# Dealing TensorE's units by VectorE's load in a graph attention kernel on one Trainium2 core

## The chip, the cores and the metric

The kernel runs on one core of a Trainium2 chip. The metric is the device time of one execution in microseconds (us), lower is better; the number given for a kernel is the median of its runs. Five engines matter: TensorE (PE; its weight loads are listed apart as PEld), VectorE (DVE), ScalarE (ACT), GpSimd (POOL, which here issues all indirect DMAs) and SyncE (SP, which issues plain DMAs).

## The reference

One layer of attention over a sparse graph, with residual and normalisation, all float32. The input x is 16 graphs of 1024 nodes with 512 features; one adjacency matrix of 1024 x 1024 zeros and ones serves all graphs.

```python
q = (x @ Wq + bq).reshape(b, n, H, HD)      # H = 8 heads of 64
k = (x @ Wk + bk).reshape(b, n, H, HD)
v = (x @ Wv + bv).reshape(b, n, H, HD)
scores = einsum('bqhd,bkhd->bhqk', q, k) / sqrt(HD)
scores = scores + (1.0 - adj) * -1e9
attn = softmax(scores, axis=-1)
out = einsum('bhqk,bkhd->bqhd', attn, v).reshape(b, n, d)
y = x + out @ Wo + bo
result = (y - mean(y)) / sqrt(var(y) + 1e-5)
```

Few entries of adj are one, so the kernel works by edges: it gathers the k and v rows of each query's neighbours and never forms the full score matrix.

## The kernel before, in words

**Tiles and blocks.** Queries are sorted by degree and cut into eight tiles of 128 (t = 0 to 7) for each of the 16 graphs ("batches", b). Tile t has OWN[t] own blocks (L27), each holding one neighbour of each of the 128 queries; tiles 6 and 7 have BLOCKS[t] further table blocks (1 and 5, L28) for the queries with more neighbours, whose results are added up by a matmul. Tile 1 (ONE_KEY, L36) holds queries with one neighbour: its attention is the gathered v row itself, so it has no block. A batch has 34 blocks (NBT), the list `blocks` (L934) has 544.

**Places.** The program is written out as places, `n` from -34 to 543 and some beyond (loop at L1165), one block to a place; the order of emission is the order on each engine's queue. In place n, `exponentials(n+3)` (ACT), `products(n+4)` (DVE, L991), the gathers for block n+8 (POOL, L970), `weigh(n+1)` on DVE (L1019) or `weigh(n+2)` on ACT (L1015, eight instructions), `add_own(n)` (DVE, L1031) and `scores(n+4)` (DVE, L995) are emitted. After a tile's last block comes `normalise` (L1043) and then `turn` (L1070), which transposes the tile on PE (L1074) and copies it out on ACT (L1078). Steps that belong to later places are put in `plan` (`later`, early in a place) or `rest` (`later_last`, after ACT's weights).

**TensorE's units.** All projections are cut into units of a known price in us of PE (PRODUCT 0.86 for a 128 x 128 x 512 product; L53). `fronts` is the list of units that make q, k and v of later batches (k and v of a pair of tiles by a seven-product scheme, L746); `finish` (L827) makes the four products with Wo (L629) for a tile that is done. Each place adds `share` to `credit` and units are emitted while credit is positive; a finish goes ahead of fronts, and starts at most once in two places. Inside a batch `share` is a constant (L1177); it is set anew for each place only in the last batches (L1171), and is LAST_SHARE once fronts is empty. What is left of credit is cut to one share (L1239).

**A finish's steps.** After the last product, `out` (L837) adds residual and bias on DVE (L852, L853, the latter with the row sum), and then, by place: `centre` (+1, DVE L858: minus the mean), `spread` (+2, in `rest`; ACT L862: squares around the mean and their sum), `variance` (+3, DVE L865), `power` (+4, POOL L868), `shift` (+5, DVE L871), `norm_out` (+6, ACT L874) and the store (+8, POOL L878). These are the steps while fronts is not empty ("single"); later, two tiles share one power instruction.

**The lead.** In places -34 to -1 the first batch's q, k, v are made while `ranks` (L370) sorts the nodes: row sums of adj on ACT (L382), a key for each node, PE broadcasts the keys (L392), DVE counts smaller keys for one tile of nodes at a time (L405, eight times), shifts the ranks so that the one-edge tile falls on its place (L411 to L417), casts them (L418), and POOL scatters (node, degree) to the table `order` in DRAM by rank (L399, eight indirect DMAs). SP loads the sorted table as `ranked` (L422), DVE casts its first column to `asked_row` (L434), which all later gathers by node use. Then `edges` (L462) makes the lists of neighbours on DVE for each tile. `loads` (L300) fetches weights on ACT's DMA queue and writes zero rows to DRAM from the tiles `zero` and `zeros` (L293, L295), which take both buffers of the tag that q uses (L658).

**Buffers named below.** Tag "qt" has Q_BUFS = 4 buffers, for the gathered query rows of table blocks (L966) and for V1, the v rows of tile 1 (L949). Y_BUFS is 6, and `load_y` (L1206) is held back while five tiles are in flight.

Of the kernel before, what the change touches and what calls it, by code (L numbers as in the profile page):

```python
# [10 lines left out]
F32 = mybir.dt.float32  # L11
# [6 lines left out]
HEADS = 8  # L18
# [12 lines left out]
AHEAD = 8  # L31
KG_BUFS, Q_BUFS, QT_BUFS, PV_BUFS, Y_BUFS = 8, 4, 3, 5, 6
NO_ROW = 65536.0
CODE, ROUND = 2048.0, 12582912.0

LONE, ONE_KEY = 64, 1  # L36

# [126 lines left out]
def kernel(  # L164
# [69 lines left out]
    with ExitStack() as main:  # L234
# [59 lines left out]
        nc.gpsimd.memset(zero, 0.0)  # L294
        zeros = work.tile([P, D], F32, tag="q", name="zeros", bufs=2)  # L295
        nc.gpsimd.memset(zeros, 0.0)
# [3 lines left out]
        def loads():  # L300
# [14 lines left out]
            for i in range(ROWS):  # L315
                nc.scalar.dma_start(kv_rows[i][N:N + 1, 0:D], zero)
                if i:
                    nc.scalar.dma_start(q_rows[i][ds(ONE_KEY * P, P), :], zeros)
            nc.vector.tensor_scalar(before, place[:, 0:P], -1.0, query[:, 0:1], op0=OP.add, op1=OP.is_gt)
# [42 lines left out]
        def later(k, fn):  # L362
            plan.setdefault(now[0] + k, []).append(fn)
# [6 lines left out]
        def ranks():  # L370
# [27 lines left out]
            def scatter(t):  # L398
                nc.gpsimd.indirect_dma_start(  # L399
                    out=order_views[t], out_offset=bass.IndirectOffsetOnAxis(ap=rank_row[:, t:t + 1], axis=0),  # L400
                    in_=asked[:, t, :], in_offset=None,
                )

            for t in range(NT):
                nc.vector.scalar_tensor_tensor(  # L405
                    keys, row, key[:, t:t + 1], place[:, 0:1].to_broadcast([P, N]), op0=OP.is_lt, op1=OP.min, accum_out=rank[:, t:t + 1]
                )
                if t % 3 == 2:
                    yield

            for at, by in ((LONE, LONE), (LONE + P, -LONE - P), (2 * P, P)):  # L411
# [3 lines left out]
                else:  # L415
                    nc.vector.tensor_tensor(moved, moved, key, op=OP.add)
            nc.vector.tensor_tensor(rank, rank, moved, op=OP.add)  # L417
            nc.vector.tensor_copy(rank_row, rank)  # L418
            for t in range(NT):
                scatter(t)  # L420
            yield
            nc.sync.dma_start(ranked, order.rearrange("(t p) c -> p t c", p=P))  # L422
            nc.vector.tensor_scalar(key, query, 1.0, None, op0=OP.add)
            nc.vector.scalar_tensor_tensor(key, rank, CODE, key, op0=OP.mult, op1=OP.add)
            nc.vector.tensor_copy(keys.rearrange("p (t q) -> p t q", t=NT), key[:, :, None].to_broadcast([P, NT, P]))
# [401 lines left out]
        def finish(b, t):  # L827
# [9 lines left out]
            def out(p):  # L837
# [18 lines left out]

                def centre():
                    nc.vector.tensor_scalar(st[:, 1:2], st[:, 0:1], -1.0 / D, None, op0=OP.mult)  # L858

                def spread():  # L860
                    sq = work.tile([P, D], F32, tag="ysq", name=f"ysq_{b}_{t}", bufs=1)
                    nc.scalar.activation(sq, y, AF.Square, bias=st[:, 1:2], accum_out=st[:, 2:3])  # L862

                def variance():
                    nc.vector.tensor_scalar(st[:, 2:3], st[:, 2:3], 1.0 / D, EPS, op0=OP.mult, op1=OP.add)  # L865

# [3 lines left out]
                def shift():  # L870
                    nc.vector.tensor_tensor(st[:, 4:5], st[:, 3:4], st[:, 1:2], op=OP.mult)  # L871

# [10 lines left out]

                later(1, centre)
                later_last(2, spread)
                later(3, variance)
                if single:
                    later(4, power)
                    later(5, shift)
                    later_last(6, norm_out)  # L890
                elif second:
                    mate_shift, mate_norm_out = half.pop()[1]

# [12 lines left out]
                    later_last(7, norm_out)  # L906
                else:
                    mine = half[0]
                    mine.append((shift, norm_out))
# [34 lines left out]
        def gather(n):  # L944
            b, t, i = blocks[n]
            assert t in listed
            if t == ONE_KEY + 1 and i == 0:
                g = NS + own[ONE_KEY]
                V1[b] = work.tile([P, D], F32, tag="qt", name=f"v1_{b}", bufs=Q_BUFS)  # L949
                nc.gpsimd.indirect_dma_start(  # L950
                    out=V1[b], out_offset=None, in_=kv_rows[b % ROWS],
                    in_offset=bass.IndirectOffsetOnAxis(ap=keys_of(b)[:, g:g + 1], axis=0), element_offset=D,
                )
# [188 lines left out]

        total = len(blocks)
        prep = {}
        for t in range(NT):
# [5 lines left out]
        with tc.manual_schedule():  # L1151
# [13 lines left out]
            while n < total or plan or rest or urgent or done or finishing or spilled or not guarded:  # L1165
# [25 lines left out]
                if 1 <= n <= total and (n == total or blocks[n][2] == 0):  # L1191
                    normalise(*blocks[n - 1][:2])
                if 0 <= n < total and blocks[n][1:] == (ONE_KEY + 1, 1):
                    turn(blocks[n][0], ONE_KEY, V1.pop(blocks[n][0]))
# [4 lines left out]
                for fn in rest.pop(n, ()):  # L1199
                    fn()  # L1200
                credit += share
                if 0 <= n < total and blocks[n][2] >= OWN[blocks[n][1]]:
# [10 lines left out]
                while credit > 0 or urgent:  # L1213
# [68 lines left out]
```

## Time and profile before

| | us |
|---|---|
| median of 3 runs | 1985.66 |
| lowest and highest | 1980.79, 1988.05 |
| the profiled execution, own time | 1981.95 |
| its span, first to last instruction | 1980.2 |

| engine | busy us | share of the span | instructions |
|---|---|---|---|
| PE | 1878.0 | 95% | 5271 |
| DVE | 1746.8 | 88% | 3727 |
| ACT | 1544.4 | 78% | 6074 |
| POOL | 1282.8 | 65% | 1206 |

The mean granted TensorE clock is 0.987. The chain of work that ended last lies 58% on PE, 19% on DVE, 6% on ACT. A float32 product is recorded as two matmul records of 512 columns. A record's duration has a modelled end that reaches into the next one, so that 95% is not a share of the peak; the step from one record's start to the next in an unbroken row is what it costs.

### The profile page before, as it was taken

The numbers are of one execution on the slowest core, as the hardware profiler recorded it, in microseconds if no ns is written. First come the engines' busy times: TensorE is split into PE (matmuls) and PEld (weight loads), VectorE is DVE, ScalarE is ACT, GpSimd is POOL, SyncE is SP. The second block draws the span as 40 slices with busy tenths as digits, with TensorE's granted clock in tenths as the row PEclk, the third lists the DMA queues.
The fourth block names the chain that finished last, engine by engine and source line by source line (L and its number), as shares of the span: only waits on it lengthen the run. The fifth ranks groups of instructions, "written<-read, shape, count | busy, mean of one in ns | idle before, by whom it ended". The sixth has DMA issues, their size and how long they took to land.

```text
span 1980.2 us, 25432 instructions
## 1 busy us (share of the span) xinstructions
PE 1878.0 (95%) x5271; PEld 904.0 (46%) x5271; DVE 1746.8 (88%) x3727; ACT 1544.4 (78%) x6074; POOL 1282.8 (65%) x1206
## 2 busy tenths in 40 slices
PE   8879899999999999999999999999999999899896
PEld 4434444444544445454544445454544445444442
DVE  3599988989988998998989899998989899989894
ACT  4514887979878897978888797887879798978784
POOL 1554665767658675776758576776857576656783
PEclk9989999999999999999999999999999999999998
DMA  7598787888878787897979788897978789987983
GB/s 267 161 310 281 240 284 260 274 289 288 314 245 301 253 306 271 272 330 247 324 222 312 266 286 301 290 312 239 314 245 297 266 291 325 323 293 266 343 315 115
DMA packets 186003, 551.29 MB, mean 278 GB/s; under 512 B 31247, under 2 KB 31275, under 8 KB 185838
## 3 DMA queue, kind: packets, MB, share of 16 engines
q0 software_dynamic: 120528, 398.76, 61.4%
q1 hardware_dynamic: 62416, 145.30, 19.4%
q10 hardware_dynamic: 2894, 5.52, 0.8%
q14 instruction: 121, 0.99, 0.2%
q8 instruction: 44, 0.72, 0.2%
HBM read 433.86 MB, written 140.30 MB: 290 GB/s over the span
## 4 chain that ended last, share of the span: by engine, by line
PE 58%; DVE 19%; ACT 6%; issue 5%; DMA 3%; POOL 1%; POOLq 0%; DVEq 0%; ACTq 0%
PE po L629 15%; PE pq L629 12%; PE pp L746 9%; PE z L746 7%; PE x L746 7%; DVE qk L991 4%; ACT pv L1015 4%; DVE s L995 4%; DMA kvg<-kv_rows,key_row 2%; PE poT L1074 2%; DVE pv L1031 2%; PE pxT L600 2%; PE sum L1040 2%; PE sum L1041 2%; DVE y L853 1%
## 5 line engine op out<-in xcount | busy, mean ns | idle before, releaser
L1015 ACT ACTIVATE pv<-kvg,pv 128x64 f32<-128x64 f32 x3544 | 893.1, 340 | 0.0
L970 POOL DMA_INDIRECT kvg<-kv_rows,key_row x544 | 622.0, 1143 | 388.5 <-ACT pv L1005 118.1
L629 PE MATMUL po<-wo,oT 128*128 128x512 f32 x944 | 434.6, 596 | 5.5 <-DVE y L852 5.5
L629 PE MATMUL pq<-wq,xT 128*128 128x512 f32 x904 | 426.9, 599 | 4.8 <-DVE y L852 2.4
L995 DVE TENSOR_REDUCE s<-qk 128x8 f32<-128x512 f32 x544 | 370.4, 681 | 6.9
L991 DVE TENSOR_TENSOR qk<-qt,kvg 128x512 f32<-128x512 f32 x448 | 306.9, 685 | 13.0 <-DMA kvg<-kv_rows,key_row 12.9
L629 PEld LDWEIGHTS po<-wo,oT 128*128 128x128 f32 x944 | 176.4, 191 | 209.2 <-issue 192.0
L629 PEld LDWEIGHTS pq<-wq,xT 128*128 128x128 f32 x904 | 168.5, 192 | 194.3 <-issue 174.9
L746 PE MATMUL pp<-t,s 128*128 128x512 f32 x504 | 238.7, 596 | 7.9 <-DVE s L615 7.8
L746 PE MATMUL x<-b,xT 128*128 128x512 f32 x504 | 240.3, 599 | 0.0
L1031 DVE TENSOR_TENSOR pv<-pv,pv 128x520 f32<-128x520 f32 x336 | 233.6, 695 | 2.6 <-ACT pv L1015 2.6
L1005 ACT ACTIVATE pv<-s,absent 128x8 f32<-128x8 f32 x448 | 131.0, 294 | 66.7 <-DVE s L995 65.6
L800 POOL DMA_INDIRECT x<-in_x_dram,asked_row x120 | 128.9, 1074 | 78.7 <-PE pxT L600 42.5
L878 POOL DMA_INDIRECT out_dram<-y,asked_row x128 | 148.9, 1163 | 36.4 <-issue 20.5
L639 ACT ACTIVATE sq_k<-kv 128x128 f32<-128x128 f32 x512 | 150.8, 301 | 18.6 <-DVE kv L769 18.6
L1078 ACT COPY oT<-poT 128x512 f32<-128x512 f32 x128 | 73.8, 577 | 104.8 <-PE po L629 99.0
L746 PEld LDWEIGHTS pp<-t,s 128*128 128x128 f32 x504 | 94.7, 191 | 120.5 <-issue 108.7
L746 PEld LDWEIGHTS x<-b,xT 128*128 128x128 f32 x504 | 96.5, 193 | 113.9 <-issue 109.5
L800 POOL DMA_INDIRECT y<-in_x_dram,asked_row x102 | 115.4, 1131 | 31.1 <-issue 26.3
L746 PE MATMUL z<-b,s 128*128 128x512 f32 x252 | 122.1, 608 | 13.0 <-DVE kv L774 13.0
L940 POOL DMA_INDIRECT qg<-q_rows,query_row x96 | 104.1, 1084 | 36.1 <-issue 24.3
L746 PE MATMUL pp<-t,xT 128*128 128x512 f32 x252 | 118.5, 592 | 1.7 <-DVE q L659 1.7
(221 smaller groups left out, 2663.9 us busy)
## 6 DMA issues: line engine op xcount, KB each, us to landing
kv_rows<-kv SPq DMA_DIRECT2D x128, 512.0 KB
q_rows<-q SPq DMA_DIRECT2D x113, 256.0 KB
qt<-q_rows SPq DMA_DIRECT2D x105, 256.0 KB
kvg<-kv_rows,key_row POOLq DMA_INDIRECT x544, 6.0
residual<-y_sorted SPq DMA_DIRECT2D x26, 256.0 KB
y<-residual SPq DMA_DIRECT2D x26, 256.0 KB
adj<-in_adj_dram POOLq DMA_DIRECT2D x8, 512.0 KB, 11.9
spill<-oT SPq DMA_DIRECT2D x10, 256.0 KB
```

Of the source, the lines that this page charges most:

```text
L629: nc.tensor.matmul(p, lhs(c), w[:, c, :], start=(c == 0), stop=(c == NPAIR - 1))
L639: nc.scalar.activation(sq, s[:, ts(h, P)], AF.Square, scale=scale, accum_out=sums[:, h:h + 1])
L746: nc.tensor.matmul(R[bank], l[:, ts(c, P)], right[:, c, :], start=(first and c == 0), stop=(c == 1), skip_group_check=True,)
L800: nc.gpsimd.indirect_dma_start(out=y, out_offset=None, in_=x_rows, in_offset=bass.IndirectOffsetOnAxis(ap=asked_row[:, t:t + 1], axis=0), ...
L878: nc.gpsimd.indirect_dma_start(out=out_rows[b, t], out_offset=bass.IndirectOffsetOnAxis(ap=asked_row[:, t:t + 1], axis=0), in_=y, in_offse ...
L940: nc.gpsimd.indirect_dma_start(out=q, out_offset=None, in_=q_rows[b % ROWS], in_offset=bass.IndirectOffsetOnAxis(ap=rows, axis=0))
L970: nc.gpsimd.indirect_dma_start(out=KG[n], out_offset=None, in_=kv_rows[b % ROWS], in_offset=bass.IndirectOffsetOnAxis(ap=keys_of(b)[:, g:g ...
L991: nc.vector.tensor_tensor(QK[n], q, KG[n][:, 0:D], op=OP.mult)
L995: nc.vector.tensor_reduce(S[n], QK.pop(n).rearrange("p (h d) -> p h d", d=HD), axis=AX.X, op=OP.add)
L1005: nc.scalar.activation(PV[n][:, D:], S.pop(n), AF.Exp, bias=bias)
L1015: nc.scalar.activation(pv[:, ts(h, HD)], v[:, ds(D + h * HD, HD)], AF.Copy, scale=pv[:, D + h:D + h + 1])
L1031: nc.vector.tensor_tensor(PV[b, t], PV[b, t], pv, op=OP.add)
```

## The change

1. The one-edge tile's V1 is gathered with block (7, 0) of its batch in place of (2, 0), and turned in the place of block (7, 4) in place of (2, 1). Q_BUFS goes from 4 to 5.
2. In places 0 to 543, `credit` gets `paced(share, n)` in place of `share`: share times the load of the place over the mean load of its batch. The load counts VectorE's large instructions of the attention in that place: 2 for products and scores, 1 if the next block is weighed on DVE, 1 for add_own, and for a tile's first block 3 or 1.3 for the normalisation of the tile before. The rest of credit is cut to two shares.
3. `centre` is gone. `spread` takes the row sum itself as its bias with scale -512 and moves from +2 to +1; `variance` divides by 512 cubed, `shift` divides the sum by -512 in one three-operand instruction. While fronts is not empty, variance stays at +3, power at +4, shift goes from +5 to +6, norm_out from +6 to +7; once it is empty, single tiles do variance, power, shift and norm_out one place sooner than before (+2, +3, +4, +5).
4. In `ranks`, each tile's ranks are cast and scattered right after the next tile's count; the table in DRAM then lies in plain rank order, and the move of the one-edge tile is made by loading `ranked` in four DMAs. The shift of the ranks for the code follows afterwards.
5. `zeros` moves from q's tag to the tag "pv0".

```diff
-KG_BUFS, Q_BUFS, QT_BUFS, PV_BUFS, Y_BUFS = 8, 4, 3, 5, 6
+KG_BUFS, Q_BUFS, QT_BUFS, PV_BUFS, Y_BUFS = 8, 5, 3, 5, 6
-LONE, ONE_KEY = 64, 1
+LONE, ONE_KEY, ONE_KEY_AT = 64, 1, (7, 4)
-        zeros = work.tile([P, D], F32, tag="q", name="zeros", bufs=2)
+        zeros = work.tile([P, D + HEADS], F32, tag="pv0", name="zeros", bufs=3)
...
                 nc.vector.scalar_tensor_tensor(
                     keys, row, key[:, t:t + 1], place[:, 0:1].to_broadcast([P, N]), op0=OP.is_lt, op1=OP.min, accum_out=rank[:, t:t + 1]
                 )
+                if t:
+                    nc.vector.tensor_copy(rank_row[:, t - 1:t], rank[:, t - 1:t])
+                    scatter(t - 1)
                 if t % 3 == 2:
                     yield
+            nc.vector.tensor_copy(rank_row[:, NT - 1:NT], rank[:, NT - 1:NT])
+            scatter(NT - 1)
+            yield
+            nc.sync.dma_start(ranked[:, 2:, :], order[2 * P:, :].rearrange("(t p) c -> p t c", p=P))
+            nc.sync.dma_start(ranked[0:LONE, 0, :], order[0:LONE, :])
+            nc.sync.dma_start(ranked[LONE:, 0, :], order[LONE + P:2 * P, :])
+            nc.sync.dma_start(ranked[:, ONE_KEY, :], order[LONE:LONE + P, :])
...
-            nc.vector.tensor_tensor(rank, rank, moved, op=OP.add)
-            nc.vector.tensor_copy(rank_row, rank)
-            for t in range(NT):
-                scatter(t)
-            yield
-            nc.sync.dma_start(ranked, order.rearrange("(t p) c -> p t c", p=P))
+            nc.vector.tensor_tensor(moved, rank, moved, op=OP.add)
...
-                def centre():
-                    nc.vector.tensor_scalar(st[:, 1:2], st[:, 0:1], -1.0 / D, None, op0=OP.mult)
-
                 def spread():
...
-                    nc.scalar.activation(sq, y, AF.Square, bias=st[:, 1:2], accum_out=st[:, 2:3])
+                    nc.scalar.activation(sq, y, AF.Square, bias=st[:, 0:1], scale=-float(D), accum_out=st[:, 2:3])
...
                 def shift():
-                    nc.vector.tensor_tensor(st[:, 4:5], st[:, 3:4], st[:, 1:2], op=OP.mult)
+                    nc.vector.scalar_tensor_tensor(
+                        st[:, 4:5], st[:, 0:1], -1.0 / D, st[:, 3:4], op0=OP.mult, op1=OP.mult
+                    )
...
-                later(1, centre)
-                later_last(2, spread)
-                later(3, variance)
+                later_last(1, spread)
                 if single:
-                    later(4, power)
-                    later(5, shift)
-                    later_last(6, norm_out)
+                    late = 1 if fronts else 0
+                    later(2 + late, variance)
+                    later(3 + late, power)
+                    later(4 + 2 * late, shift)
+                    later_last(5 + 2 * late, norm_out)
                 elif second:
+                    later(3, variance)
...
-            if t == ONE_KEY + 1 and i == 0:
+            if (t, i) == (ONE_KEY_AT[0], 0):
...
+        def load_of(n):
+
+            b, t, i = blocks[n]
+            had = 2.0 + (not by_act(min(n + 1, total - 1))) + (0 < i < OWN[t])
+            if i == 0:
+                had += 3.0 if BLOCKS[blocks[n - 1][1]] else 1.3
+            return had
+
+        def paced(share, n):
+            b0 = min(n // NBT, B - 1) * NBT
+            return share * load_of(n) * NBT / sum(load_of(m) for m in range(b0, b0 + NBT)) if n < total else share
...
-                if 0 <= n < total and blocks[n][1:] == (ONE_KEY + 1, 1):
+                if 0 <= n < total and blocks[n][1:] == ONE_KEY_AT:
                     turn(blocks[n][0], ONE_KEY, V1.pop(blocks[n][0]))
...
-                credit += share
+                credit += paced(share, n) if n >= 0 else share
...
-                credit = min(credit, share)
+                credit = min(credit, 2 * share)
```

More of the change, by code (lines that the diff above doesn't have):

```diff
@@ L317, in loads @@
                 if i:
-                    nc.scalar.dma_start(q_rows[i][ds(ONE_KEY * P, P), :], zeros)
+                    nc.scalar.dma_start(q_rows[i][ds(ONE_KEY * P, P), :], zeros[:, 0:D])
             nc.vector.tensor_scalar(before, place[:, 0:P], -1.0, query[:, 0:1], op0=OP.add, op1=OP.is_gt)
@@ L416, in ranks @@
                     nc.vector.tensor_tensor(moved, moved, key, op=OP.add)
-            nc.vector.tensor_tensor(rank, rank, moved, op=OP.add)
-            nc.vector.tensor_copy(rank_row, rank)
-            for t in range(NT):
-                scatter(t)
-            yield
-            nc.sync.dma_start(ranked, order.rearrange("(t p) c -> p t c", p=P))
+            nc.vector.tensor_tensor(moved, rank, moved, op=OP.add)
             nc.vector.tensor_scalar(key, query, 1.0, None, op0=OP.add)
-            nc.vector.scalar_tensor_tensor(key, rank, CODE, key, op0=OP.mult, op1=OP.add)
+            nc.vector.scalar_tensor_tensor(key, moved, CODE, key, op0=OP.mult, op1=OP.add)
             nc.vector.tensor_copy(keys.rearrange("p (t q) -> p t q", t=NT), key[:, :, None].to_broadcast([P, NT, P]))
@@ L855, in out @@
                 )
-                def centre():
-                    nc.vector.tensor_scalar(st[:, 1:2], st[:, 0:1], -1.0 / D, None, op0=OP.mult)
                 def spread():
                     sq = work.tile([P, D], F32, tag="ysq", name=f"ysq_{b}_{t}", bufs=1)
-                    nc.scalar.activation(sq, y, AF.Square, bias=st[:, 1:2], accum_out=st[:, 2:3])
+                    nc.scalar.activation(sq, y, AF.Square, bias=st[:, 0:1], scale=-float(D), accum_out=st[:, 2:3])
                 def variance():
-                    nc.vector.tensor_scalar(st[:, 2:3], st[:, 2:3], 1.0 / D, EPS, op0=OP.mult, op1=OP.add)
+                    nc.vector.tensor_scalar(st[:, 2:3], st[:, 2:3], 1.0 / D ** 3, EPS, op0=OP.mult, op1=OP.add)
                 def power():
@@ L907, in out @@
                 else:
+                    later(3, variance)
                     mine = half[0]
```

## The prediction

> **What bounds the kernel now.** I read the page's first part, then the busy times by stage, then who waited for whom in each stage, then the timeline where a wait stood out. The stages are cut at the scores reductions of line 995 that open batch 0, batch 1, batch 13 and at the last one. Columns: stretch, its us, busy us and instructions of PE, PEld, DVE, ACT, POOL, clock, DMA share, GB/s.
>
> ```profile
> 0.00:75.20 75.20, 61.28 (x179) 29.88 (x179) 31.87 (x65) 35.97 (x83) 18.49 (x35) 1.00 0.54 194
> 75.20:156.60 81.40, 69.86 (x167) 31.06 (x168) 67.24 (x211) 23.20 (x80) 49.96 (x51) 0.92 0.89 304
> ...
> 290.50:1653.20 1362.70, 1337.21 (x3786) 646.32 (x3785) 1246.67 (x2562) 1131.39 (x4516) 937.48 (x873) 1.00 0.84 283
> 1653.20:1946.20 293.00, 270.00 (x749) 130.29 (x748) 270.00 (x576) 248.25 (x982) 188.38 (x164) 0.98 0.87 304
> ```
>
> PE's busy time overstates its work, since a record's end is modelled. The chain of work has "384.67 3.43 PE po L629 x8": 0.429 us a record in an unbroken row. Transposes step 0.109 (eight from 46.46 to 47.33 in the timeline), the two records of a sum 0.216 and 0.220. Multiplying the counts of the groups by form: batches 1 to 12 hold 2746 records of 512 columns, 752 transposes, 144 pairs of sum records: 1178 + 82 + 63 = 1323 us of work in 1362.7, so PE stands 40 us. The same sum gives 259 of 293 in batches 13 to 15 (34 idle), 121 of 134 in batch 0 (13 idle), 119 of 156.6 in the lead (37 idle). PE bounds the middle, its work is the same after the change, and the prize is those idle stretches. In batches 13 to 15 DVE is busy 270 of 293: there both bind.
>
> Who makes PE and DVE stand in the middle (engine, line, who ended the wait, us in all, times, longest):
>
> ```profile
> DVE stats L865 <- ACT ysq L862: 49.0, 24, 4.9
> DVE qk L991 <- DMA kvg<-kv_rows,key_row: 14.1, 12, 3.4
> DVE stats L871 <- POOL stats L868: 9.1, 11, 2.3
> ...
> PE po L629 <- DVE y L852: 5.5, 3, 2.1
> PE z L746 <- DVE kv L774: 3.9, 3, 1.8
> PE poT L1074 <- DVE y L852: 3.6, 5, 2.1
> ```
>
> One case shows how a DVE wait becomes a PE wait (start, us, instruction, idle before it and who ended it):
>
> ```profile
> 893.65 0.59 ACT L1078 COPY oT<-poT 128x512 f32<-128x512 f32 x1 [7.24 <-PE po L629]
> ...
> 896.53 0.71 ACT L862 ACTIVATE ysq<-y,stats 128x512 f32<-128x512 f32 x1
> ...
> 897.37 0.15 DVE L865 TENSOR_SCALAR stats<-stats 128x1 f32<-128x1 f32 x1 [4.88 <-ACT ysq L862]
> ...
> 901.31 3.70 PE L629 MATMUL po<-wo,oT 128*128 128x512 f32 x8 [2.11 <-DVE y L852]
> ```
>
> ACT stands in front of the oT copy because PE has other units before the transposes; the squares stand behind that copy; variance, one place later, stops DVE; and DVE then frees a PSUM buffer late.
>
> In the lead one wait stands out:
>
> ```profile
> 57.59 1.07 POOL L399 DMA_INDIRECT order<-asked,rank_row  x1 [45.83 <-DVE s L614]
> ...
> 66.87 0.96 POOL L399 DMA_INDIRECT order<-asked,rank_row  x1 [0.30 <-issue]
> ...
> 70.57 0.37 SPq L422 DMA_DIRECT2D ranked<-order  x1
> ...
> 74.34 0.17 DVE L434 CAST asked_row<-ranked 128x8 int32<-128x8 f32 x1 [9.81 <-DMA ranked<-order]
> ...
> 75.17 1.11 PE L600 MATMUL pxT<-ident,x 128*128 128x128 f32 x4 [5.45 <-DVE q L659]
> ...
> 76.08 2.96 PE L746 MATMUL z<-t,s 128*128 128x512 f32 x4
> ```
>
> The eight scatters go out only after the last count, 1.27 us apart; the sorted table is asked for 3.7 us after the last, and is there 3.8 us later. DVE stands in front of it, and PE behind DVE.
>
> **The Trainium skill.** "Perfetto Trace Analysis", Identifying the Most-Contended Engine, says that matmul busy time is no measure of the distance from the peak; the trace agrees (1337 busy, 1323 worked). "TensorE: Matmul & The Clock Gate", Part 1, says that an idle PE falls to half clock for about a window of 3.4 us; after the 5.45 us the four z records take 2.96 where unbroken ones take 1.88. The same part calls ACT and DVE strict first-in first-out: the squares behind the oT copy show it. "VectorE: DVE Perf Modes", SBUF-src ops, prices a DVE instruction at 58 cycles and one per element, an estimate of 61 ns for one element: the stats instructions at 1930.68 and 1930.74 step 60.
>
> **The change, part by part.**
>
> Ranks and scatter. Each scatter leaves after the next count. Counts end at 55.11; seven more casts of 0.08 (56.59 to 56.67) put the last at 55.7; the last cast to its scatter takes 1.0 as now (56.59 to 57.59): 56.7. Landing 3.7: 60.4. Four issues of 0.37 on SP in place of one: the last at 61.5. Then 3.8: asked_row at 65.3. POOL stood idle from 11.8 to 57.6, so the scatters pass nothing; q_rows and kv_rows writes queued behind `ranked` on SP (71.04, 71.66) leave earlier too. DVE is through with its work before the cast at 64.5, 65.1 with the casts. So 9.8 of wait becomes 0.2, and PE, busy to 69.7, no longer stops: 5.45 + (2.96 - 1.88) = 6.5 us. After it PE is unbroken to 110 and DVE's lists follow (10 us of small DVE waits on PE between 75 and 100 take the shift). **Value -6.5; ends -3 (the four small loads take 3 us longer) and -9.8.**
>
> Zeros. DVE waits 19.19 us at 29.88 for the zero rows. PE runs from 9 to 69 with 1.8 us of holes in that stretch, and the ranking starts from a key at 37.60 that needs ACT's row sums, over at 36.47. That cover hides it: 0, at most -1.1.
>
> No centre. 128 DVE instructions of 0.06 are 7.7 us of DVE, in the middle beside PE's work. Where DVE binds, some 28 tiles finish after 1653: 1.7 us, counted with the end. The three-operand shift costs as the two-operand one (0.15; L460, three-operand, takes 0.16).
>
> Spread one place earlier, variance two places after it, shift two after power. The squares now precede the oT copy that held them. In the case shown DVE goes on at 892.4 with vsum and qk to 894.4, and the next add_own (L1031) needs ACT's weights that end at 896.5: 2.1 of 4.88 us come back as another wait, 57% are saved. PE waits on y are 5.5 + 3.6 + 2.4 (pq) = 11.5 of the 25.4 listed; the other 14.6 of PE's 40 idle are mostly half clock after such waits, 6.6 of them in proportion. 18.1 x 0.57 = **-10**. Norm_out and store one place later hold y some 3 us longer: fifteen places, at 4.25 places a tile 3.5 in flight under the limit of five; 0.
>
> Dealing by load. By the formula a middle batch has a mean load 3.16: factor 1.58 in places (0, 0) and (7, 0), 1.27 before a block weighed on DVE, about 1 at most own blocks, 0.63 at table blocks. A batch has 28 x 1.72 + 28 x 0.86 + 8 x 0.44 of fronts, 27.5 of finishes, 5.2 of sums: a share of 3.19, so 5.0 units in the heavy places and 2.0 in light ones. No instruction is added. PE then has work queued where DVE is long, and DVE less of PE's output to take in there beside its own. It addresses the remaining PE waits (z, sum, pm, pxT): 13.9 listed + 8.0 clock = 22. The trace doesn't show such pacing: from all of it (-22) to a loss of 10. **Value a third, -7.** In batches 13 to 15 PE stands most in front of poT (13.5, behind the normalising DVE) and sum (6.7). PE gets units there, but DVE has only 23 idle us: a quarter of it, with 1.7 of centre, **-7; ends -16 and +6**. Batch 0: **-1**.
>
> One-edge tile. Same instructions: four transposes, a copy, four products, and in the light places of t = 7, where no tile finishes now. V1's gather (1.1 us on POOL) moves to places without gathers of table queries; V1 then stays while five of those come, which the fifth "qt" buffer covers; without it POOL would wait some places for V1. In the last batch the tile comes eight places before the end, where a finish starts every second place anyway: 0, at most +4 (one more finish, 3.4 us, after the last). Effect counted with the dealing.
>
> Sum: -6.5 - 10 - 7 - 7 - 1 = -31.5. From the profiled 1981.95 that is 1950.5; the median shown is 3.7 above it, so 1985.66 - 31.5 = **1954** for the median.
>
> **The rivals.** (a) *Only the lead moves.* PE's middle is 97% worked; waits just change their names (variance's becomes add_own's) and the dealing gains nothing. For: every remaining wait is small. Against: PE stops right behind DVE's stops. 1985.66 - 6.5 = 1979. (b) *Transposes pushed back*, slower. In (0, 0) and (7, 0) PE gets 1.85 us more units ahead of the transposes of the tile just normalised; ACT already waits 97.8 us there (26 times, up to 7.4), and its weights stand behind. If that comes through in full at 32 places: +59, less the lead's 6.5: 2038; I take half, 30 - 6.5: 2009. It decides from 0.5 us a place on (16 us repay the lead and make 0.5%). Against: PE works meanwhile, so only what later stops PE counts. (c) The scatters might not leave early if each waits for all counts; then the forecast loses its 6.5: 1960, inside the forecast's own range (0.05 of its chance).
>
> **How the numbers follow.** The forecast has 0.72 (own range 1935 to 1975), rival (a) 0.16, (b) 0.12. 0.5% (9.9 us) is about what a measurement of this kernel can tell from no change: faster 0.72, same 0.16, slower 0.12. All gains at their ends would give 1926; the range 1928 to 1990 leaves out a little below, and above it (b).
>
> **What would show it.** Right: no DVE wait on `ranked` over 2 us and the first scores reduction near 150 in place of 156.6; variance's wait on ysq under 15 us in all; a batch of the middle 112 us in place of 113.6; PE's idle in the middle under 25. Wrong: ACT's waits on PE before oT grown well over 98 us, or L1031 waiting on ACT for 30 or more; PE idle at table blocks in front of the sums, since they now get fewer units.

## The result, and the profile after

The changed kernel took 1953.27 us (median of 4 runs, 1952.06 to 1955.2) against 1986.86 us for the kernel before on the same chip: ratio 0.9834, 95% interval 0.9807 to 0.9862, so faster by 1.4 to 1.9%. The forecast was 1954. Its profiled execution took 1952.72 us, with a span of 1951.0 against 1980.2. The page's first part gives, for each engine, busy time, share of the span and instructions:

```profile
PE 1871.4 (96%) x5275; PEld 903.7 (46%) x5275; DVE 1741.1 (89%) x3604; ACT 1550.1 (79%) x6074; POOL 1295.9 (66%) x1205
```

DVE has 123 instructions fewer (centre is gone; the ranks are now cast one tile at a time) and 5.7 us less to do. PE has the same work. I took PE's idle time record by record, as the prediction did: the step from one matmul's start to the next, less 0.429, 0.109, 0.216 or 0.220 us by its form. Records that only step more slowly, without a stop before them, count as idle in this sum too. Before, the steps hold 126.9 us of idle time in 1980.2; after, 97.8 in 1951.0. What is left is 1853.3 and 1853.2 us. So all 29 us of the gain between the two profiles are PE standing or stepping slowly for less time, and the question is which part of the change did it, and where.

The windows view of the changed kernel, cut as before at the scores reductions that open the batches (times, length, then busy us and count for PE, PEld, DVE, ACT, POOL, then granted clock, DMA share, GB/s):

```profile
0.00:153.70 153.70, 131.32 (x347) 61.06 (x348) 101.19 (x281) 59.77 (x166) 70.33 (x86) 0.96 0.74 254
153.70:284.70 131.00, 124.49 (x359) 59.45 (x358) 122.34 (x273) 97.75 (x409) 79.24 (x73) 1.00 0.82 273
284.70:1631.20 1346.50, 1333.73 (x3794) 647.81 (x3793) 1241.54 (x2464) 1137.30 (x4519) 944.64 (x873) 1.00 0.85 287
1631.20:1916.00 284.80, 264.89 (x736) 126.76 (x735) 266.90 (x553) 246.78 (x970) 192.04 (x165) 0.98 0.90 307
1916.00:1951.00 35.00, 17.00 (x47) 8.62 (x45) 9.16 (x38) 8.49 (x15) 9.61 (x11) 0.80 0.22 78
```

The middle (third line) is 1346.5 us for 1362.7 before: 112.2 a batch, where 112 was forecast. The lead is 153.7 for 156.6, batches 13 to 15 take 284.8 for 293.0.

Who makes DVE stand in the middle now (engine, line, who ended the wait, us in all, times, longest):

```profile
DVE g L770 <- PE pp L751: 14.9, 17, 2.5
DVE y L857 <- PE po L634: 10.2, 13, 1.5
DVE qk L998 <- DMA kvg<-kv_rows,key_row: 7.5, 6, 2.6
```

The 49.0 us of variance behind the squares, which led this list, have left it. DVE now waits mostly for PE, as is to be expected in a stretch that PE bounds. The same view for PE:

```profile
PE sum L1047 <- DVE pv L1026: 3.8, 3, 2.7
PE z L751 <- DVE kv L779: 2.6, 2, 2.5
PE sum L1047 <- DVE qk L998: 2.0, 1, 2.0
```

The waits behind `y` are gone, and the sums of the table blocks have come to the top: one of the signs that the prediction named against itself, though small.

### The profile page after: what moved, and what is told of

Its sections match the earlier page's. It is cut to its first block, busy times and chain, and to the rows that moved or that the text cites. A ratio compares the mean times of both kernels' runs of the same rounds, so it can differ in the third digit from the quotient of the medians.

```text
span 1951.0 us, 25391 instructions
## 1 busy us (share of the span) xinstructions
PE 1871.4 (96%) x5275; PEld 903.7 (46%) x5275; DVE 1741.1 (89%) x3604; ACT 1550.1 (79%) x6074; POOL 1295.9 (66%) x1205
## 5 line engine op out<-in xcount | busy, mean ns | idle before, releaser
L977 POOL DMA_INDIRECT kvg<-kv_rows,key_row x544 | 623.6, 1146 | 330.9 <-issue 101.2
L634 PE MATMUL pq<-wq,xT 128*128 128x512 f32 x904 | 422.5, 598 | 1.7 <-DVE q L664 1.3
L805 POOL DMA_INDIRECT x<-in_x_dram,asked_row x120 | 135.8, 1132 | 89.0 <-PE pxT L605 62.2
L805 POOL DMA_INDIRECT y<-in_x_dram,asked_row x102 | 113.4, 1112 | 30.8 <-issue 29.0
L751 PE MATMUL z<-t,s 128*128 128x512 f32 x252 | 118.6, 593 | 0.0
```

What stands on the lines that cost most here:

```text
L634: nc.tensor.matmul(p, lhs(c), w[:, c, :], start=(c == 0), stop=(c == NPAIR - 1))
L751: nc.tensor.matmul(R[bank], l[:, ts(c, P)], right[:, c, :], start=(first and c == 0), stop=(c == 1), skip_group_check=True,)
L805: nc.gpsimd.indirect_dma_start(out=y, out_offset=None, in_=x_rows, in_offset=bass.IndirectOffsetOnAxis(ap=asked_row[:, t:t + 1], axis=0), ...
L977: nc.gpsimd.indirect_dma_start(out=KG[n], out_offset=None, in_=kv_rows[b % ROWS], in_offset=bass.IndirectOffsetOnAxis(ap=keys_of(b)[:, g:g ...
```

## The experiments

A letter for a theory holds only within the run whose expectation defines it, or within its group. All ratios are to the kernel before, run on the same chip in the same stretch of time; it took 1982.44, 1987.25, 1980.91 and 2003.48 us in the four groups, so ratios are compared, not times. The table puts the profiled executions side by side, each one execution of a kernel, and on different chips: stages in us; PE's idle time in batches 1 to 12; over the whole run, ACT's wait on PE before the oT copy and DVE's wait on the squares before variance.

| kernel | ratio | lead | batch 0 | 1 to 12 | 13 to 15 | tail | PE idle 1 to 12 | oT wait | squares wait |
|---|---|---|---|---|---|---|---|---|---|
| before | 1 | 156.6 | 133.8 | 1362.7 | 293.0 | 34.0 | 40.3 | 102.7 | 57.8 |
| after | 0.9834 | 153.7 | 131.0 | 1346.5 | 284.8 | 35.0 | 23.4 | 23.1 | 0.9 |
| b_finish | 0.9881 | 157.2 | 134.9 | 1340.8 | 292.2 | 32.0 | 18.5 | 91.4 | 0.9 |
| b_pace | 0.9932 | 155.9 | 129.1 | 1357.9 | 288.0 | 32.3 | 33.1 | 107.4 | 45.6 |
| b_tile | 0.9857 | 156.8 | 127.6 | 1336.3 | 290.8 | 36.6 | 12.9 | 15.2 | 15.2 |
| b_scatter | 0.9983 | 152.0 | 136.6 | 1362.2 | 291.1 | 32.3 | 41.4 | 102.8 | 58.1 |
| a_tile_back | 0.9854 | 155.0 | 127.9 | 1357.1 | 289.3 | 31.9 | 30.8 | 101.2 | 0.9 |
| a_finish_back | 0.9794 | 152.6 | 129.9 | 1347.5 | 283.6 | 35.4 | 24.5 | 22.5 | 14.6 |
| a_no_pace | 0.9823 | 155.5 | 132.6 | 1339.7 | 291.6 | 35.1 | 19.8 | 12.8 | 0.9 |
| a_best | 0.9787 | 149.5 | 131.7 | 1346.5 | 284.1 | 35.2 | 23.6 | 24.0 | 0.9 |
| c_lead | 0.9813 | 149.5 | 128.1 | 1336.0 | 295.0 | 36.7 | 12.9 | 15.2 | 15.4 |
| c_spot | 0.9841 | 157.5 | 128.2 | 1336.4 | 291.8 | 34.0 | 14.0 | 14.7 | 20.4 |
| c_end | 0.9764 | 149.2 | 128.5 | 1333.2 | 285.8 | 36.2 | 11.0 | 16.8 | 15.1 |

One further run, b_gap, has its profile from the chip on which the kernel before took 2003.48 us, so its stages are not in the table.

How far a stage can be trusted is seen where kernels have the same, or nearly the same, code in it. The middle repeats within 0.5 us (before and b_scatter; b_tile and c_lead), the lead within 2.4 (a_finish_back, after, a_tile_back: 152.6 to 155.0), batch 0 within 3 (before 133.8, b_scatter 136.6), batches 13 to 15 within about 4 (b_tile 290.8, c_lead 295.0) and the tail within 2 (before 34.0, b_scatter 32.3). Smaller differences say little.

### One part at a time

**The finish steps alone** (part 3 of the change, on the kernel before):

```diff
...
-                later(1, centre)
-                later_last(2, spread)
-                later(3, variance)
+                later_last(1, spread)
                 if single:
-                    later(4, power)
-                    later(5, shift)
-                    later_last(6, norm_out)
+                    late = 1 if fronts else 0
+                    later(2 + late, variance)
+                    later(3 + late, power)
+                    later(4 + 2 * late, shift)
+                    later_last(5 + 2 * late, norm_out)
...
```

> The kernel before with the finish's steps of the change alone (no centre, squares one place earlier, shift and norm_out later). Theory F, the finish's waits held PE back: DVE's wait on ysq falls from 57.8 to under 5 us and the time by about 10 to 13 us, nearly all in batches 1 to 12. Rival N, waits only change names: ysq's wait goes, but DVE's wait in front of line 1031 (add_own, on ACT's weights) or on PE's products rises by as much, and the time falls by under 3 us.

Measured: 1957.94 us, ratio 0.9881 [0.9862, 0.99], some 24 us. DVE's wait on the squares goes from 57.8 to 0.9 us and the middle gives 21.9 us, twice what was expected. ACT's wait before the oT copy, though, is still there (middle of the kernel before, then of b_finish):

```profile
ACT oT L1078 <- PE po L629: 97.8, 26, 7.4
...
ACT oT L1080 <- PE po L629: 85.4, 28, 7.4
```

So ACT may stand there, and most of the loss is gone all the same. It suggests that what cost time was the squares behind that wait and DVE behind the squares; the run called "only the gap", below, gives a reason to doubt that this is all that the finish steps do.

**The dealing alone** (part 2):

```diff
...
-                credit += share
+                credit += paced(share, n) if n >= 0 else share
...
-                credit = min(credit, share)
+                credit = min(credit, 2 * share)
```

> The kernel before with the dealing by load alone (paced share, credit cut at two shares). Theory F gives it a part of the rest: 5 to 12 us less, over batches 1 to 12 and 13 to 15 together. Rival D, the dealing made the whole gain: 20 us or more less. Rival T, transposes pushed back: slower by 5 us or more, with ACT's waits in front of the oT copy well over 99 us.

Measured: 1968.01 us, 0.9932 [0.9915, 0.9948]. The middle gives 4.8 us, batch 0 4.7, batches 13 to 15 5.0, as theory F expected; both rivals, a gain of 20 us or a loss of 5, are out. Over the run ACT's wait before the oT copy stays (102.7 us before, 107.4 here); DVE's on the squares goes from 57.8 to 45.6. The bound on what is left of credit applies in the lead too.

**The one-edge tile alone** (part 1):

```diff
-KG_BUFS, Q_BUFS, QT_BUFS, PV_BUFS, Y_BUFS = 8, 4, 3, 5, 6
+KG_BUFS, Q_BUFS, QT_BUFS, PV_BUFS, Y_BUFS = 8, 5, 3, 5, 6
-LONE, ONE_KEY = 64, 1
+LONE, ONE_KEY, ONE_KEY_AT = 64, 1, (7, 4)
...
-                if 0 <= n < total and blocks[n][1:] == (ONE_KEY + 1, 1):
+                if 0 <= n < total and blocks[n][1:] == ONE_KEY_AT:
...
```

> The kernel before with the one-edge tile turned in the place of block (7, 4) alone, with five buffers for tag qt. Theory F counts it as a help to the dealing, 0 to 5 us less. If it makes the gain by itself (one finish less at the crowded start of a batch, where ACT waits for oT): 8 us or more less, and DVE's wait on ysq falls well under 58 us without any change of the steps. If the last batch pays for the late tile, up to 4 us more after the last scores reduction.

Measured: 1952.62 us, 0.9857 [0.9834, 0.988]. This is the surprise of the study: the part that I had put at nothing does by itself what the whole change does. The middle falls to 1336.3 us, PE's idle time there from 40.3 to 12.9. The run has the fifth qt buffer as well as the new place. In the same view of the middle of b_tile, ACT's line on po is gone and one on the transposes themselves remains:

```profile
ACT oT L1078 <- PE poT L1074: 14.9, 15, 1.5
```

**The scatters alone** (part 4, zeros not moved):

```diff
...
+                if t:
+                    nc.vector.tensor_copy(rank_row[:, t - 1:t], rank[:, t - 1:t])
+                    scatter(t - 1)
...
```

> The kernel before with the scatter of the change alone; zeros stay in q's tag. As predicted, 6.5 us less, with the first scores reduction at about 150 in place of 156.6. The changed kernel gained only 3 us there, and two things stood in the way: the counts began at 44.96 in place of 42.98, and a DVE shift instruction beside POOL's memset took 2.29 us in place of 0.17. If the first is the zeros' doing, the counts here begin at about 43 and the gain is 4 to 5 us; if it is not, about 3 us as in the changed kernel. The long shift instruction should be there in both cases.

Measured: 1978.61 us, 0.9983 [0.9975, 0.9992]: some 4 us, in the lead (156.6 to 152.0).

The four single gains add up to about 72 us; the whole change gave some 33. Three of the four draw on the same idle time: at places 8 to 14 of a batch PE stands for 21.2 us in the middle of the kernel before, for 0.3 with the tile moved, 2.2 with the finish steps and 9.1 with the dealing.

### One part left out

**The tile put back** into the changed kernel:

```diff
-KG_BUFS, Q_BUFS, QT_BUFS, PV_BUFS, Y_BUFS = 8, 5, 3, 5, 6
+KG_BUFS, Q_BUFS, QT_BUFS, PV_BUFS, Y_BUFS = 8, 4, 3, 5, 6
...
-                if 0 <= n < total and blocks[n][1:] == ONE_KEY_AT:
+                if 0 <= n < total and blocks[n][1:] == (ONE_KEY + 1, 1):
```

> The changed kernel with the one-edge tile turned at block (2, 1) again, four qt buffers; the rest of the change stays. Theory T (the tile's crowding at the start of a batch is what made ACT stand before oT, and the finish steps and the dealing only work around the same stall): with the crowding back, the finish steps still cut it: slower than the changed kernel by 0 to 8 us, ACT's wait before oT back over 70 us, DVE's wait on ysq still under 10. Theory A (the parts add up): slower by 25 to 32 us, as much as the tile alone gained. Theory P (the dealing is what costs the parts their sum): by 5 to 15, since the dealing stays.

Measured: 1961.09 us, 0.9854 [0.9828, 0.988]: by the profiles 10 us longer than the changed kernel, by the ratios some 4, with intervals that overlap. Nearly all of the 10 are in the middle (1357.1 for 1346.5). ACT's wait is back (middle of a_tile_back), and since the finish steps keep the squares ahead of it, DVE's is not:

```profile
ACT oT L1085 <- PE po L634: 81.2, 22, 7.6
```

Theory A, that parts add up, is out: at most 10 us and not 25 to 32. Theory T expected up to 8 and has the waits right; theory P's 5 to 15 covers the time as well, so this run doesn't part these two.

**The finish steps put back** (the first diff reversed in the changed kernel):

> The changed kernel with the finish steps of before (centre on DVE, spread two places after, variance one after that); tile, dealing, scatters and zeros stay. Theory T: within 5 us of the changed kernel, DVE's wait on ysq 10 to 25 us and nothing else. Theory A: slower by 20 to 27. Theory P: within 5, since what costs is the dealing. A variant, theory G (the two-place gap is itself what costs beside the tile): faster by 5 to 10 in the middle.

Measured: 1949.7 us, 0.9794 [0.9768, 0.982]; the middle 1347.5 against 1346.5. Beside the tile and the dealing, the finish steps are worth nothing that shows. A is out again, G too (it wanted a middle shorter by 5 to 10).

**The dealing left out** of the changed kernel (the second diff reversed):

> The changed kernel with the plain share in every place and credit cut to one share; tile, finish steps, scatters and zeros stay. Theory P: faster by 5 to 12 us, the middle near the 1336 us of the tile alone. Theory T: within 5. Theory A: slower by 10 to 17. My theory of the prediction (dealing worth a third of the other waits): slower by 5 to 10.

Measured: 1955.46 us, 0.9823 [0.9796, 0.9849]. Over the whole it makes no difference, but the stages do differ: without the dealing the middle is 6.8 us shorter (1339.7), and batches 13 to 15 are 6.8 us longer (291.6). Theory P has the middle nearly right and the sum wrong; the difference in batches 13 to 15 is not far above what the same code gives in two profiles.

**Zeros back, checks later**, everything else as in the changed kernel:

```diff
-        zeros = work.tile([P, D + HEADS], F32, tag="pv0", name="zeros", bufs=3)
+        zeros = work.tile([P, D], F32, tag="q", name="zeros", bufs=2)
...
-        prep.setdefault(-22, []).append(checks())
+        prep.setdefault(-20, []).append(checks())
```

> The changed kernel with the zero rows back in q's tag and the checks (whose two POOL MEMSETs of adj run beside DVE's shift of the ranks) one unit list later. If the zeros' move costs the lead: counts start near 43.0 in place of 44.96, 1.5 to 2 us of the lead back. If the POOL memset is what makes one DVE instruction take 2.29 us: it takes 0.17 and another 0 to 2 us come back, the lead at 150 to 151.5. Else: the lead stays at 153.7, the time within 2 us of the changed kernel.

Measured: 1948.5 us, 0.9787 [0.9761, 0.9813], and a lead of 149.5 in place of 153.7. In four profiles with the zeros moved and the checks early the lead took 152.6 to 155.5, in the three without both 149.2 to 149.5. The two causes can be seen in the timeline (start, us, engine or its queue, line, instruction, idle time before it and who ended it). The changed kernel:

```profile
14.85 8.30 SPq L665 DMA_DIRECT2D q_rows<-q  x2
...
22.66 3.34 ACTq L316 DMA_DIRECT2D kv_rows<-zero  x2
...
28.84 0.59 ACT L669 COPY kv<-pk 128x512 f32<-128x512 f32 x1 [9.76 <-DMA q_rows<-q]
...
41.06 0.17 DVE L386 SCALAR_TENSOR_TENSOR key<-asked,query 128x8 f32<-128x8 f32 x1 [10.25 <-ACT adj L382]
...
44.96 1.28 DVE L405 SCALAR_TENSOR_TENSOR keys<-key_of,key,place 128x1024 f32<-128x1024 f32 x1 [1.66 <-ACT key_of L395]
...
60.21 2.29 DVE L422 TENSOR_SCALAR key<-rank 128x8 f32<-128x8 f32 x1
...
60.62 1.86 POOL L454 MEMSET adj<- 128x1024 f32 x2
...
68.47 0.16 DVE L439 CAST asked_row<-ranked 128x8 int32<-128x8 f32 x1
```

And the version with zeros back and checks later:

```profile
19.04 0.82 ACTq L316 DMA_DIRECT2D kv_rows<-zero  x2
...
24.23 0.59 ACT L669 COPY kv<-pk 128x512 f32<-128x512 f32 x1 [5.03 <-PE pk L723]
...
30.61 1.12 SPq L665 DMA_DIRECT2D q_rows<-q  x2
...
37.63 0.16 DVE L386 SCALAR_TENSOR_TENSOR key<-asked,query 128x8 f32<-128x8 f32 x1
...
42.94 1.28 DVE L405 SCALAR_TENSOR_TENSOR keys<-key_of,key,place 128x1024 f32<-128x1024 f32 x1 [3.23 <-ACT key_of L395]
...
58.20 0.38 DVE L422 TENSOR_SCALAR key<-rank 128x8 f32<-128x8 f32 x1
...
65.21 0.17 DVE L439 CAST asked_row<-ranked 128x8 int32<-128x8 f32 x1 [0.59 <-DMA ranked<-order]
```

With zeros in their new place, q's rows are free early, so q's write to DRAM goes out at 14.85, among the weight loads, and its two issues take 8.30 us instead of 1.12. ACT's zero rows come 3.6 us later and its copy of kv 4.6, the row sums behind that copy too, the key 3.4 us later, the counts 2.0. The scatters alone, without the zeros' move, start the counts at 43.17: the move is what costs these 2 us. Then L422 takes 2.29 us where its like takes 0.17, beside two POOL memsets that moved up when the scatters went ahead; with the checks later it takes 0.38. The scatters alone, whose zeros are not moved, show the same long instruction:

```profile
58.07 2.60 DVE L422 TENSOR_SCALAR key<-rank 128x8 f32<-128x8 f32 x1
58.79 1.86 POOL L454 MEMSET adj<- 128x1024 f32 x2
```

### Versions made from what was found

**Tile, scatters and later checks only** on the kernel before (the diffs of these three above):

> The kernel before with three parts only: the tile turned at (7, 4) with five qt buffers, the scatters one by one, and the checks one list later; centre, finish steps and share as before, zeros in q's tag. If what the trace of the other runs says holds stage by stage: lead 149.5 to 150.5 (as in the changed kernel with zeros and checks put back), batch 0 128, batches 1 to 12 1336, batches 13 to 15 290, tail 36: 1940 profiled, 11 us faster than the changed kernel, ratio to before 0.978 to 0.981. If the finish steps or the dealing carry part of the change's gain themselves: 1950 or more.

Measured: 1944.24 us, 0.9813 [0.9797, 0.9829]; 1945.3 profiled where 1940 was expected. Lead (149.5), batch 0 (128.1) and middle (1336.0) are as expected; batches 13 to 15 take 295.0 instead of 290, in a profiled execution that was the slowest of five (1947.33 us; the others 1943.78 to 1944.28). The middle's gain is there without the finish steps and the dealing.

**The tile elsewhere**, in the kernel before with nothing else changed; the lines show the difference to the tile alone:

```diff
-LONE, ONE_KEY, ONE_KEY_AT = 64, 1, (7, 4)
+LONE, ONE_KEY, ONE_KEY_AT = 64, 1, (5, 2)
```

> The kernel before with only the one-edge tile moved, but to block (5, 2), place 13, between the tiles done at places 11 and 16, gathered with (5, 0). Theory S (what counts is that the turns at places 0, 2, 3, 4, 7 of a batch are thinned to 0, 2, 4, 7; where the tile goes matters little): 1952 to 1960, ACT's wait before oT under 40, DVE's on ysq under 25. Theory W (what counts is that the tile's products fall into the wide hole of places 22 to 33, in which PE lacked work): most of the gain gone, 1968 or more, PE idle of the middle near 30.

Measured: 1949.58 us, 0.9841 [0.9824, 0.9858]; middle 1336.4. At place 13, among own blocks, the tile's move does as much as at place 26. Theory S is right: it is the start of the batch that was too full, and the places of t = 7, in which no other tile finishes, are not what the tile needed.

**The dealing from batch 13 on only**, and the last batch's tile back at (2, 1), on the version with tile, scatters and later checks; the lines show the difference to that version:

```diff
...
-            if (t, i) == (ONE_KEY_AT[0], 0):
+            if (t, i) == (ONE_KEY_AT[0] if b < B - 1 else 2, 0):
...
-                credit += share
+                credit += paced(share, n) if n >= 13 * NBT else share
...
-                credit = min(credit, share)
+                credit = min(credit, share if n < 13 * NBT else 2 * share)
...
```

> As the version with tile, scatters and late checks, with the dealing from batch 13 on only, and in the last batch the tile turned at (2, 1) as before. Stage by stage: the middle stays at 1336; batches 13 to 15 go from 290 to 284 (what the dealing gave them in the whole change: 7 to 8); the tail goes from 36 back to 32: 1930 to 1934 profiled, ratio to before 0.973 to 0.977. If the crowding in the last batch costs what it saves in the tail: 1935 or more, with batch 15 longer.

Measured: 1934.06 us, 0.9764 [0.9748, 0.978], the fastest version, and its interval lies below the whole change's. Its windows, from the lead to the tail:

```profile
0.00:149.20 149.20, 129.02 (x345) 60.04 (x346) 98.98 (x281) 58.98 (x163) 69.24 (x85) 0.97 0.76 263
...
277.70:1610.90 1333.20, 1328.66 (x3784) 646.92 (x3784) 1246.78 (x2561) 1136.12 (x4521) 944.13 (x874) 1.00 0.85 289
1610.90:1896.70 285.80, 264.52 (x746) 127.13 (x744) 269.83 (x579) 246.61 (x974) 195.07 (x167) 0.99 0.89 310
1896.70:1932.90 36.20, 18.64 (x47) 9.71 (x47) 10.19 (x43) 9.09 (x17) 9.22 (x11) 0.74 0.21 75
```

The end was expected to go from 290 to 284. It gives 9.2 us against the version with tile, scatters and later checks (295.0 to 285.8) and 5.0 against the tile alone (290.8). The tail did not come back to 32, so its length is not the late tile's doing alone.

**Only the gap**, on the kernel before: centre and spread as before, the steps after them later, those of tiles that share a power instruction too. Variance is two places after spread, as in the finish steps; but every step from spread on comes one place later than there, norm_out at +8 in place of +7.

```diff
-                later(3, variance)
+                later(4, variance)
...
-                    later(4, power)
-                    later(5, shift)
-                    later_last(6, norm_out)
+                    later(5, power)
+                    later(7, shift)
+                    later_last(8, norm_out)
...
```

> The kernel before with its centre step and the spread two places after the finish, as before, and only variance, power, shift and norm_out later: variance two places after spread in place of one. Theory Q (the stop of DVE before variance is what the finish steps removed, 1 place more is enough): as the finish steps alone, ratio 0.987 to 0.990, DVE's wait on ysq under 5, PE idle of the middle under 22. Theory E (the earlier spread, ahead of the oT copy, or the 128 instructions less are what counts): 0.993 to 1.000, DVE's wait on ysq gone but PE idle of the middle above 30.

Measured: 1993.28 us against 2003.48, 0.9949 [0.9924, 0.9973]. DVE's wait on the squares is gone (1.5 us), and only half a per cent is gained, where the finish steps as a whole gave 1.2% with an interval that doesn't touch this one. PE's idle time at places 8 to 14 did go (21.2 us before, 2.9 here), but its sum in the middle stayed (40.7), with 24.2 us at places 22 to 33. All three marks of theory E are met, which says that the earlier squares, or the 128 instructions less, carry part of the gain. It is not shown, for two reasons. The later norm_out may itself cost time, which no run tells apart. And the kernel before has no profile from this chip: 9.3 of the 24.2 us are three single stops of 2.0 to 4.5 us, each in another batch, so they are no regular part of the schedule.

## Why the forecast's number held and several of its steps did not

**What the wait before oT is.** The prediction said that ACT stands there "because PE has other units before the transposes". That is the step that failed. The timeline of the kernel before, just ahead of the case that the prediction shows:

```profile
887.86 0.60 PE L1074 MATMUL poT<-ident,o 128*128 128x128 f32 x4
...
890.02 3.60 PE L629 MATMUL po<-wo,oT 128*128 128x512 f32 x8
```

The transposes are over at 888.46. The copy starts at 893.65, 0.04 us after the product with Wo of another tile. All 25 such waits of over 1 us in the middle (97.3 us) end 0.04 us after the last matmul record of a po, each time that of the tile four before in order of copying, with the own transposes over for 2.6 us or more. At each of them three earlier tiles had still to get their product with Wo when the copy began: it was always the fourth copy in flight, and line 1077 gives the tag oT `LAZY + 2`, that is four buffers. The copy waits for the buffer of the tile four before it, still read by PE. It is a full ring, not PE's order. The program helps to fill it: while `fronts` is not empty, a finish starts only when more than LAZY = 2 tiles are copied and waiting.

**Why the tile mattered.** In the kernel before, tiles are turned in places 0, 2, 3, 4 and 7 of a batch, then 11, 16 and 22; the one-edge tile is the one at 3. Five copies come in eight places, and each finish takes eight matmul records of 0.43 us and at least two places, so at most four start in that time. (Below, an instant counts to place n when the last scores reduction that DVE has begun is that of block n+3; steps of PE that are too long by a few hundredths of a us are left out.) Of 99.4 us of oT wait in the middle, 92.6 lie in places 7 to 11; of 49.0 us of DVE's wait on the squares, 36.4; and of 38.4 us of PE's idle time, 21.2 lie in places 8 to 14. With the tile alone moved these are 3.7 of 14.9, 0.4 of 11.8 and 0.3 of 11.9; moved to place 13, 4.2, 0.3 and 0.3. So what hangs on the ring's stall at one spot of the batch was more than half of PE's idle time in the middle. The tile takes the stall away; the finish steps leave it (82.6 us) and take the squares out from behind it; doing both pays once. A run with five oT buffers in the kernel before, or with five qt buffers alone, was not made: that the ring is the cause is shown by what ended the waits and by two places of the tile, not by its size, and a share of the fifth qt buffer in the tile's gain is not ruled out by a run.

Now the steps in turn.

- **Lead, -6.5: measured -2.9.** The mechanism is right: the wait on `ranked` is gone. The start was mis-sized, not the chain: counts began 2 us late and L422 took 2 us. Without these two the cast lies at 65.21 (forecast 65.3) and the lead is 149.5 ("near 150"), 7.1 us gained, in a_best.
- **Zeros, 0: wrong, about +2.** "That cover hides it" priced the wait that goes, and not where the write it releases goes. That write's queue was part of the chain to the key.
- **No centre: right** that it is little: 5.7 us of DVE's busy time in place of 7.7, in the changed kernel.
- **Finish steps, -10: the direction right, the size wrong both ways.** The wait on the squares goes, as forecast. Alone the steps give -21.9 in the middle; the return as a wait of add_own was 6 us (2.6 to 8.8) and not 43% of 49, and how much of the rest is due to the earlier squares or the missing instructions stays open. In company of the tile and the dealing they give -1.0.
- **Dealing, -7 in the middle: wrong in company.** Alone -4.8; beside tile and finish steps +6.8 (1339.7 to 1346.5). The prediction's sign for it came: sums of table blocks wait 5.8 us. (By the formula four of a batch's six table blocks have the factor 0.63; the other two have 0.95.) That is not all of it, and where the rest arises isn't settled: with the dealing and the old finish steps PE's idle time is 24.5 too, but spread over other places. **-7 in batches 13 to 15: right**, as far as stages that repeat within 4 us can tell: -5.0 alone and -6.8 in company. Batch 0, -1: -4.7 alone and -1.6 in company, neither far from what the same code gives in two profiles.
- **One-edge tile, 0: the term that was missed.** Alone -26.4 in the middle and -6.2 in batch 0; put in last, -10.6 in the middle. The tail is 3 us longer with it (36.6 for 34.0; 35.0 for 31.9 with the tile put back), within the +4 allowed, but the run that put the last batch's tile back kept a long tail, so that this is the tile's doing is not shown.
- **The sum.** The middle was forecast at -17 and gave -16.2, the end -7 and gave -8.2, the lead gave 3.6 less and batch 0 1.8 more. The middle's figure came out because I took the idle time as the prize and half of it as won, which bounds any mix of these parts; the division among them was wrong. That the terms added up to the right number was luck: one that was put at nothing gives nearly the whole alone, and three share one prize.
- **The rivals.** (a) is out: the waits did not only change names, PE's idle time fell by 17 us in the middle. (b) is out: what would decide it was never PE's order. Its fair test is the dealing alone, with the tile where it was: the oT wait grew only from 102.7 to 107.4 us, and the kernel became faster. In the changed kernel the wait fell to 23 us, which is the tile's doing. (c) is out: in the changed kernel the first scatter leaves at 48.47 us, while the counts run to 57.2.

## What to carry to other kernels

When an engine waits for "a matmul", look at whether its own input was long ready: if it was, suspect a wait for a buffer to come free and see whose reading ends it. Moving one tile to a quieter place can be worth as much as reordering everything behind the stall. Place waits by their position in the loop, not only by line: a cost in five of 34 places points to what is crowded there, and edits that each relieve the same spot must not be added. When a wait is removed early in a kernel, follow the transfer that it held back, since it may leave at a worse time.

## What was not expected of the hardware

- A DVE TENSOR_SCALAR of 128x8 took 2.29 and 2.60 us, in place of 0.17, while POOL ran two MEMSETs of 128x1024; without them beside it, 0.38. The Trainium skill, "SBUF — State Buffer", Terms, says of the port pair that DVE and GpSimd share that it is held for the full instruction and that "the loser fully blocks"; the ends agree with that, since both long instructions end 0.02 us after the second MEMSET; but by the records they began 0.41 and 0.72 us before the first, and no run shows the port itself.
- Two plain DMA issues on SP took 8.30 us among the weight loads (DMA share 1.04 from 14.8 to 23.2 in the changed kernel) and 1.12 us when they came sixteen us later (share 0.29 from 30.6 to 31.8 in the version with zeros back and checks later).
- One kernel's median was 1980.91 to 2003.48 us on the chips used here, more than two of the four parts of this change are worth alone.
